# Graph layer: 30 tiles of source rows by single DMAs from two queues, bulk loads on ScalarE's queue, 391 picks instead of 400

## Chip, cores and metric

One core of a Trainium2 chip. The metric is the device time of the kernel in microseconds, as the median of several executions; a profiled execution of the kernel before, with its own time, is read besides.

## What is computed

One message-passing layer of a graph network with 6250 nodes, 200,000 edges (sorted by target node), and 64 features:

```python
w = silu(edge_attr @ W1 + b1) @ W2 + b2              # 200000 x 9
h_src = x[src]                                       # 200000 x 64, a gather
msg = einsum('ef,em,fmg->eg', h_src, edge_sh * w, W_tp)
agg = segment_sum(msg, dst, N) / sqrt(E / N)
emb = silu(c_noise[:, None] @ Wn1 + bn1) @ Wn2 + bn2
gamma, beta = split(emb, 2)
out = layernorm(x + agg * (1 + gamma) + beta)
```

## The kernel before

The edges are cut into 1563 tiles of 128, and 16 tiles make a block (98 blocks, the last one of 11 tiles). For a tile, a window matmul (line 728, in `windows`) multiplies the 128 source rows, as weights, with the weighted spherical harmonics spread over 7 nodes of a window. So every tile needs its 128 rows of `x`, 256 bytes each, with an edge on each partition. There are three ways to get them:

- *Gather*: GpSimd's indirect DMA (line 126, in `gather`), one instruction for a tile. It fetches 1158 tiles.
- *Pick*: TensorE (line 683, in `pick`). The table `x` lies in SBUF as two f32r halves; a one-hot matrix of the source numbers (`hots`, line 668 on VectorE, from keys `kr` that are loaded with a bulk DMA) multiplies it in 14 matmuls of 448 columns, and VectorE masks and reduces the result (lines 693, 696). 400 tiles: five in every ninth block, four in the others (`picked`).
- *Rows one by one*: ScalarE's queue issues a DMA for each row (line 154, in `load_rows`), with the address from a register. One tile in every 16th block, five tiles in all (`APG`), eight rows in a block.

The loop over `i` is written out by hand, and each engine runs its instructions in that order. In iteration `i` TensorE picks for block `i + 1` and, in `middle(i)`, runs the first layer of block `i + 2` (`hidden`, line 609), the second layer of block `i + 1` (`second`, line 633) and the windows of block `i`. GpSimd gathers for block `i + 2` behind marks ("beats") in TensorE's matmuls. Every fourth block is a finishing block (23 of them): two output blocks are normalized, with a square root on ScalarE (line 1039, with its table load) behind that block's rows; the next iteration begins with the placing of sums (line 813), the copy of the carry on ScalarE (line 819), `yt` on VectorE (line 822), and then the first layer.

SyncE's queue carries the bulk loads: at the top of odd iterations the edge attributes `ea` (512 KB for two blocks), harmonics `sh` (144 KB) and keys `kr` (320 KB), every fourth iteration also the node scalars `cb` and the store of two finished blocks:

```python
if i % LB == 1 and i + 1 + LB < NBLK:
    load(i + 1 + LB)
    load_keys(i + 1 + LB)
if i % 4 == 3 and i + 1 < NJ:
    gate_load(i + 1)
```

Each DMA counts on a semaphore from one pool for SyncE and ScalarE, and a new DMA on a semaphore first waits for the one before it there.

## Time and profile before

| what | value |
|---|---|
| three runs | 1475.52, 1476.37, 1476.50 us; median 1476.37 |
| profiled execution | 1476.88 us, its span 1474.5 us |
| TensorE (PE) busy | 1458.9 us, 99% of the span |
| VectorE (DVE) busy | 1257.2 us, 85% |
| GpSimd (POOL) busy | 1097.9 us, 74% |
| ScalarE (ACT) busy | 504.9 us, 34% |
| DMA | 98.27 MB, 67 GB/s mean |

The span runs from the first to the last instruction; the 2.4 us between it and the execution's time lie outside of it. A row of the timeline has start, duration, engine, line, operation and operands, then the idle time in front of it and what ended it. PE is the matmul pipe, PEld the weight loads beside it; ACTq and SPq are DMA issues of ScalarE's and SyncE's queues, which are not counted as busy. Matmuls overlap, so the chain (each piece up to where the next one takes over) tells what a stretch of them costs, not their durations.

### The profile page before, as it was taken

The numbers are of one execution on the slowest core, as the hardware profiler recorded it, in microseconds if no ns is written. First come the engines' busy times: TensorE is split into PE (matmuls) and PEld (weight loads), VectorE is DVE, ScalarE is ACT, GpSimd is POOL, SyncE is SP. The second block draws the span as 40 slices with busy tenths as digits, with TensorE's granted clock in tenths as the row PEclk, the third lists the DMA queues.
The fourth block names the chain that finished last, engine by engine and source line by source line (L and its number), as shares of the span: only waits on it lengthen the run. The fifth ranks groups of instructions, "written<-read, shape, count | busy, mean of one in ns | idle before, by whom it ended". The sixth has DMA issues, their size and how long they took to land.

```text
span 1474.5 us, 32845 instructions
## 1 busy us (share of the span) xinstructions
PE 1458.9 (99%) x12002; PEld 1266.0 (86%) x12002; DVE 1257.2 (85%) x2222; ACT 504.9 (34%) x1413; POOL 1097.9 (74%) x1167
## 2 busy tenths in 40 slices
PE   7999999999999999999999999999999999999998
PEld 6888888888888888888888888888888888888886
DVE  8988898798888888979879898888798888987886
ACT  5332333242333333333424233333242333333333
POOL 7777777777777777777777777777777777777773
PEclk9999999999999999999999999999999999999999
DMA  7413222221222212312222122122221222222211
GB/s 214 105 55 87 59 75 60 68 75 41 75 68 60 75 42 74 83 45 74 58 64 72 39 76 71 50 74 57 62 73 40 74 65 56 75 56 64 57 28 23
DMA packets 85439, 98.27 MB, mean 67 GB/s; under 512 B 32100, under 2 KB 46646, under 8 KB 85270
## 3 DMA queue, kind: packets, MB, share of 16 engines
q1 hardware_dynamic: 46358, 56.29, 12.9%
q0 software_dynamic: 37056, 38.02, 11.5%
q8 instruction: 98, 1.61, 0.4%
q10 hardware_dynamic: 1856, 1.77, 0.4%
q14 instruction: 71, 0.58, 0.1%
HBM read 94.24 MB, written 1.75 MB: 65 GB/s over the span
## 4 chain that ended last, share of the span: by engine, by line
PE 95%; DVE 3%; DMA 1%; SPq 1%; issue 0%; POOL 0%; ACT 0%; POOLq 0%; DVEq 0%
PE pxw L683 75%; PE pzw L728 7%; PE p L609 4%; PE p L633 4%; PE p L797 3%; DVE hot_k L668 1%; PE p L860 1%; PE p L813 1%; PE p L828 1%; SPq L435 1%; DVE xm L693 0%; DVE hs L696 0%; PE pzw L609 0%; PE p L803 0%; DMA out_dram<-o 0%
## 5 line engine op out<-in xcount | busy, mean ns | idle before, releaser
L126 POOL DMA_INDIRECT hs<-in_x_dram,src_i x1158 | 1096.6, 947 | 355.9 <-issue 158.2
L683 PE MATMUL pxw<-xs_w,hot_k 128*128 128x448 f32 x5600 | 1165.1, 365 | 1.5 <-DVE hot_k L668 1.5
L683 PEld LDWEIGHTS pxw<-xs_w,hot_k 128*128 128x128 f32 x5600 | 1036.2, 188 | 78.3 <-ACT xs_w L351 2.3
L693 DVE SCALAR_TENSOR_TENSOR xm<-li,jl,pxw 128x448 f32<-128x448 f32 x400 | 271.0, 678 | 175.2 <-PE pxw L683 174.2
L668 DVE TENSOR_TENSOR hot_k<-kr,pxw 128x896 fp32r<-128x896 f16 x393 | 416.0, 1079 | 0.0
L696 DVE TENSOR_REDUCE hs<-xm 128x64 f32<-128x448 f32 x400 | 248.2, 620 | 13.8
L637 ACT ACTIVATE p2s<-p,b2c 128x256 f32<-128x256 f32 x98 | 46.5, 474 | 599.4 <-PE p L633 577.8
L744 ACT COPY ztw<-pzw 64x140 f32<-64x140 f32 (+1 forms) x778 | 208.8, 268 | 8.5 <-PE pxw L728 0.5
L728 PEld LDWEIGHTS pzw<-a,hs 128*64 128x64 f32 x3106 | 101.1, 138 | 29.5 <-issue 23.8
L653 DVE TENSOR_TENSOR a<-oh,p 128x1008 f32<-128x1008 f32 x98 | 118.0, 1204 | 3.3
L728 PE MATMUL pzw<-a,hs 128*64 128x63 f32 x3106 | 111.2, 224 | 0.1
L624 ACT ACTIVATE st<-pzw,b1c 128x256 f32<-128x256 f32 x196 | 82.3, 471 | 1.2
L620 ACT ACTIVATE st<-p,b1c 128x512 f32<-128x512 f32 x98 | 67.1, 685 | 38.1 <-PE p L797 33.4
L819 ACT COPY carry<-p 128x128 f32<-128x128 f32 x46 | 12.3, 266 | 167.2 <-PE p L813 165.6
L609 PE MATMUL p<-ea,w1bd 32*64 32x256 f32 x784 | 66.5, 402 | 0.9 <-DVE yt L822 0.9
L609 PE MATMUL pzw<-ea,w1bd 32*64 32x256 f32 x784 | 66.5, 402 | 0.0
L633 PE MATMUL p<-st,w2p 128*32 128x256 f32 x784 | 62.6, 391 | 0.6 <-DVE a L653 0.6
L648 DVE TENSOR_TENSOR p<-p,sh 128x72 f32<-128x72 f32 x196 | 47.3, 241 | 6.7
L633 PEld LDWEIGHTS p<-st,w2p 128*32 128x32 f32 x784 | 15.5, 107 | 37.9 <-issue 37.2
L797 PE MATMUL p<-ztw,wtc 128*64 128x224 f32 x440 | 46.5, 357 | 0.0
L644 DVE STREAM_TRANSPOSE p<-p2s 128x256 f32<-128x256 f32 x98 | 44.3, 452 | 0.0
L797 PEld LDWEIGHTS p<-ztw,wtc 128*64 128x64 f32 x440 | 29.6, 136 | 17.1 <-issue 9.1
(187 smaller groups left out, 499.1 us busy)
## 6 DMA issues: line engine op xcount, KB each, us to landing
ea<-in_ea_dram SPq DMA_DIRECT2D x48, 512.0 KB
hs<-in_x_dram,src_i POOLq DMA_INDIRECT x1158
kr<-kd SPq DMA_DIRECT2D x48, 320.0 KB
apart<-in_x_dram ACTq DMA_DIRECT2D x640, 0.2 KB
sh<-in_sh_dram SPq DMA_DIRECT2D x49, 144.0 KB
cb<-cn_d SPq DMA_DIRECT2D x12, 128.0 KB
out_dram<-o SPq DMA_DIRECT2D x23, 64.0 KB
dst_i<-in_dst_dram SPq DMA_DIRECT2D x1, 768.0 KB
```

The lines of the kernel that those rows point to most:

```text
L126: d = nc.gpsimd.indirect_dma_start(out=hs[g][:, t - g * KB, :], out_offset=None, in_=x, in_offset=bass.IndirectOffsetOnAxis(ap=src_i[:, t: ...
L609: mm = nc.tensor.matmul(half[q][s * H:(s + 1) * H].rearrange("p (c t e) -> p c t e", c=4, t=2), w1bd[q * D:(q + 1) * D, (q % 2) * H:(q % 2 ...
L624: nc.scalar.activation(st[g][:, 2 + q], pzw[q][:, 2 * P:], AF.Silu, bias=b1c)
L633: mm = nc.tensor.matmul(p2[g][c * D:(c + 1) * D, 0, :].rearrange("p (q e) -> p q e", q=4), w2p, s[:, :, c * 2 * D:(c + 1) * 2 * D], start= ...
L653: nc.vector.tensor_mul(a[g], oh_t.pop(g)[:, :, None, :].to_broadcast([P, KB, M, W]), sw.unsqueeze(3).to_broadcast([P, KB, M, W]))
L668: nc.vector.tensor_tensor(hot_k[g, t], keys[:, t, None, :].to_broadcast([P, J, P]), n_p.unsqueeze(2).to_broadcast([P, J, P]), op=ALU.is_equal)
L683: mm = nc.tensor.matmul(px.rearrange("p f l -> p (f l)"), hot_k[g, t][:, h, :], xs[i][:, h].rearrange("p f l -> p (f l)"), start=(h == 0 a ...
L693: nc.vector.scalar_tensor_tensor(xm, li[:, None, :].to_broadcast([P, F, J]), jl[:, c:c + 1], px, op0=ALU.is_equal, op1=ALU.mult)
L696: read_by[g, t] = nc.vector.tensor_reduce(hs[g][:, tiles(g) - q + t, :], xm, AX.X, ALU.add)
L728: mm = nc.tensor.matmul(pz[v][v * F:(v + 1) * F, k // 2].rearrange("p m w -> p (m w)"), apart.pop(g) if g in APG and k0 + k == 0 else hsg[ ...
L744: copy(z[h * F:(h + 1) * F, 0:5 - h, k0 + k:k0 + n:2, :].rearrange("p m k w -> p k m w"), pz[v][v * F:(v + 1) * F, k // 2:(n + 1 - v) // 2 ...
L797: mm = nc.tensor.matmul(pt[h * F:(h + 1) * F].rearrange("p (s k w) -> p s k w", s=2, k=KB), wtc2[:, c, :], z[h][:, :, c], start=(c == 0), ...
```

## The change

Ten tiles instead of five come by ScalarE's rows (every eighth block, 16 rows in a block), 20 tiles by rows that SyncE issues (tile 1 of every fourth block from 16 to 92, 32 rows in a block, begun ten blocks ahead and with three buffers). Rows of each queue count on semaphores of their own, and TensorE waits for the whole tile in front of its window matmul. The bulk loads and stores of the loop move from the top of SyncE's iteration to ScalarE's queue, behind the reads and in front of that iteration's rows. Only two blocks (5 and 53) keep a fifth pick: 391 picks, 1142 gathers.

```diff
-APS = 16
+APS = 8
+SPS, SPA = 4, 10
+SPG = range(16, NBLK - 2, SPS)
+SPR = P // SPS
...
-    return Q - 2 if g == 0 else 2 if g == NBLK - 1 else Q - (g % 9 != 5)
+    return Q - 2 if g == 0 else 2 if g == NBLK - 1 else Q - (g % 48 != 5)
...
-            due[g] = list(range(g * KB + (g in APG), g * KB + tiles(g) - picked(g)))
+            due[g] = [g * KB + k for k in range(tiles(g) - picked(g)) if not (k == 0 and g in APG or k == 1 and g in SPG)]
...
-        row_a = keep.tile([len(APG), P], I32)
+        row_a = keep.tile([len(APG) + len(SPG), P], I32)
+        fetched = [tc.alloc_semaphore(f"fetched{k}") for k in range(2)]
...
-                nc.scalar.dma_start(apart[g][e0 + k:e0 + k + 1].bitcast(U8), x8[bass.ds(vs[k], 4 * F)].unsqueeze(0))
+                d = nc.scalar.dma_start(apart[g][e0 + k:e0 + k + 1].bitcast(U8), x8[bass.ds(vs[k], 4 * F)].unsqueeze(0))
+                tc.no_tile_sem_insts.add(d.ins.name)
+                tc.add_to_no_dep_group(f"apart{g}", d.ins)
+                d.then_inc(fetched[APG.index(g) % 2], 16)
+        landed = [tc.alloc_semaphore(f"landed{k}") for k in range(3)]
+        def load_lone(i):
+            g = (i + SPA - SPG[0]) // SPS * SPS + SPG[0]
+            if g not in SPG:
+                return
+            e0 = (i + SPA - SPG[0]) % SPS * SPR
+            if e0 == 0:
+                lone[g] = gath.tile([P, F], F32, tag="lone", name=f"lone{g}", bufs=3)
...
+            for k in range(SPR):
+                d = nc.sync.dma_start(lone[g][e0 + k:e0 + k + 1].bitcast(U8), x8[bass.ds(vs[k], 4 * F)].unsqueeze(0))
...
+                d.then_inc(landed[SPG.index(g) % 3], 16)
...
-            cn_j = temp.tile([NJ, P], F32)
+            cn_j = xb.rearrange("p j f -> p (j f)")[0:NJ, NJ * F - P:]
...
+                    if g in APG and k0 + k == 0:
+                        m = APG.index(g)
+                        w = nc.tensor.wait_ge(fetched[m % 2], (m // 2 + 1) * P * 16)
+                        tc.declare_fence(w.ins, group=f"apart{g}")
+                    if g in SPG and k0 + k == 1:
+                        m = SPG.index(g)
+                        w = nc.tensor.wait_ge(landed[m % 3], (m // 3 + 1) * P * 16)
+                        tc.declare_fence(w.ins, group=f"lone{g}")
...
-                if i % LB == 1 and i + 1 + LB < NBLK:
-                    load(i + 1 + LB)
-                    load_keys(i + 1 + LB)
-                if i % 4 == 3 and i + 1 < NJ:
-                    gate_load(i + 1)
                 while tables:
                     tables.pop()()
-                while stores:
-                    stores.pop(0)()
+                load_lone(i)
...
                 for f in reads:
                     f()
+                if i % LB == 1 and i + 1 + LB < NBLK:
+                    load(i + 1 + LB, nc.scalar)
+                    load_keys(i + 1 + LB, nc.scalar)
+                if i % 4 == 3 and i + 1 < NJ:
+                    gate_load(i + 1, nc.scalar)
+                while stores:
+                    stores.pop(0)(nc.scalar)
                 load_rows(i)
```

TensorE between the windows of block 22 and the next first layer, where block 23 is picked (`hot_k_1` to `hot_k_4` are its tiles 1 to 4, `hot_k_0` is tile 0 of block 24). Before:

```order
L728 MATMUL pzw_90<-a_4373,hs_3533 64x63 x8
L683 MATMUL pxw_93<-xs_w,hot_k_1_4294 128x448 x14
L683 MATMUL pxw_91<-xs_w,hot_k_2_4308 128x448 x14
L683 MATMUL pxw_92<-xs_w,hot_k_3_4418 128x448 x14
L683 MATMUL pxw_93<-xs_w,hot_k_4_4439 128x448 x14
L683 MATMUL pxw_91<-xs_w,hot_k_0_4466 128x448 x2
```

The same place in the change:

```order
L768 MATMUL pzw_90<-a_5995,hs_4577 64x63 x8
L715 MATMUL pxw_92<-xs_w,hot_k_1_5915 128x448 x14
L715 MATMUL pxw_93<-xs_w,hot_k_2_5929 128x448 x14
L715 MATMUL pxw_91<-xs_w,hot_k_3_6070 128x448 x14
L715 MATMUL pxw_92<-xs_w,hot_k_0_6214 128x448 x2
```

One stretch of 14 matmuls is gone; this happens in ten blocks, and in block 53 one is added.

ScalarE from the last first-layer activations of block 39 on (`apart` is the tile that gets single rows). Before:

```order
L624 ACTIVATE st_7688<-pzw_89,b1c 128x256
L624 ACTIVATE st_7688<-pzw_90,b1c 128x256
L149 TENSOR_LOAD row_a
L154 DMA apart_6640<-in_x_dram 1x256 x8
```

The same place in the change:

```order
L656 ACTIVATE st_11454<-pzw_89,b1c 128x256
L656 ACTIVATE st_11454<-pzw_90,b1c 128x256
L597 DMA ea_11515<-in_ea_dram 128x2x512
L600 DMA sh_11516<-in_sh_dram 128x2x144
L621 DMA kr_11519<-kd 128x1280
L532 DMA cb_11521<-cn_d 64x512
L556 DMA out_dram<-o_11313 128x2x64
L153 TENSOR_LOAD row_a
L158 DMA apart_9687<-in_x_dram 1x256 x16
```

Five bulk DMAs now stand in front of the rows, and there are 16 rows instead of eight. On SyncE, in turn, the loop holds nothing but register loads (line 175) and 32 row DMAs (line 180) in a block, and two early stores of keys:

```order
L272 DMA kd<-kt 120x128 x2
L175 TENSOR_LOAD row_a
L180 DMA lone_1367<-in_x_dram 1x256 x32
L175 TENSOR_LOAD row_a
L180 DMA lone_1367<-in_x_dram 1x256 x32
```

The bulk loads that stood there before are gone from this engine.

## Rows read from the trace of the kernel before

**Rows 1.** The page, part 1 (busy us, share, instructions) and part 4 (chain).

```profile
PE 1458.9 (99%) x12002; PEld 1266.0 (86%) x12002; DVE 1257.2 (85%) x2222; ACT 504.9 (34%) x1413; POOL 1097.9 (74%) x1167
...
PE 95%; DVE 3%; DMA 1%; SPq 1%; issue 0%; POOL 0%; ACT 0%; POOLq 0%; DVEq 0%
```

**Rows 2.** Groups: shapes, count, busy us, mean ns, idle before and its releasers.

```profile
L683 PE MATMUL pxw<-xs_w,hot_k 128*128 128x448 f32 x5600 | 1165.1, 365 | 1.5 <-DVE hot_k L668 1.5
L126 POOL DMA_INDIRECT hs<-in_x_dram,src_i x1158 | 1096.6, 947 | 355.9 <-issue 158.2 <-PE pxw L683 92.1 <-DMA hs<-in_x_dram,src_i 58.5
L728 PEld LDWEIGHTS pzw<-a,hs 128*64 128x64 f32 x3106 | 101.1, 138 | 29.5 <-issue 23.8 <-DMA hs<-in_x_dram,src_i 3.7
```

**Rows 3.** Waits: waiter <- releaser, us in total, times, longest us.

```profile
POOL hs L126 <- issue: 158.2, 519, 0.3
ACT var L1039 <- DVE var L1038: 70.9, 23, 4.9
```

**Rows 4.** Timeline at block 4: its last gather, its first window matmuls (start, us).

```profile
80.36 0.94 POOL L126 DMA_INDIRECT hs<-in_x_dram,src_i  x1 [0.30 <-DMA hs<-in_x_dram,src_i]
...
86.77 1.15 PE L728 MATMUL pzw<-a,hs 128*64 128x63 f32 x32
```

**Rows 5.** Timeline at the end: the last gather, first window matmul of block 97.

```profile
1453.42 0.94 POOL L126 DMA_INDIRECT hs<-in_x_dram,src_i  x1 [0.30 <-issue]
...
1464.44 0.24 PE L728 MATMUL pzw<-a,hs 128*64 128x63 f32 x1
```

**Rows 6.** The chain by time, 1020 to 1100 us: runs of pick matmuls.

```profile
1028.61 14.21 PE pxw L683 x70
...
1061.03 11.41 PE pxw L683 x56
```

**Rows 7.** Timeline of ScalarE and its queue, block 38 (finishing), from the last rows.

```profile
601.88 2.18 ACTq L154 DMA_DIRECT2D apart<-in_x_dram  x7
604.09 1.28 ACT L1039 ACT_TABLE_LOAD   x1 [2.08 <-DMA apart<-in_x_dram]
608.07 0.30 ACT L1039 ACTIVATE var<-var,eps 128x2 f32<-128x2 f32 x1 [2.69 <-DVE var L1038]
608.47 0.27 ACT L819 COPY carry<-p 128x128 f32<-128x128 f32 x1
```

**Rows 8.** Timeline of SyncE's queue: two bulk loads in a row.

```profile
610.18 0.42 SPq L565 DMA_DIRECT2D ea<-in_ea_dram  x1
610.65 0.47 SPq L568 DMA_DIRECT2D sh<-in_sh_dram  x1
```

**Rows 9.** Timeline behind them: `yt` on VectorE, first-layer matmul on TensorE.

```profile
609.59 0.28 DVE L822 TENSOR_TENSOR yt<-p,carry 128x128 f32<-128x128 f32 x1
...
610.39 0.43 PE L609 MATMUL p<-ea,w1bd 32*64 32x256 f32 x2
```

**Rows 10.** ScalarE: copy in block 37; block 39's rows; next instruction.

```profile
587.53 0.33 ACT L806 COPY rt<-p 128x224 f32<-128x224 f32 x1
...
616.41 0.46 ACTq L154 DMA_DIRECT2D apart<-in_x_dram  x1
...
626.00 0.47 ACT L637 ACTIVATE p2s<-p,b2c 128x256 f32<-128x256 f32 x1 [8.78 <-DMA ea<-in_ea_dram]
```

**Rows 11.** Windows of 4 us: sum, busy by engine, TensorE clock, DMA share, GB/s.

```profile
610.00:614.00 4.00, 4.00 (x66) 2.75 (x65) 3.97 (x5) 2.20 (x3) 2.94 (x4) 1.00 0.73 208
...
618.00:622.00 4.00, 4.00 (x22) 3.75 (x21) 3.44 (x5) 0.00 (x0) 3.09 (x4) 1.00 0.19 35
622.00:626.00 4.00, 4.00 (x46) 2.90 (x46) 3.93 (x7) 0.00 (x0) 3.09 (x4) 1.00 0.80 238
```

**Rows 12.** VectorE at the start of block 38: first one-hots of new keys.

```profile
594.35 2.08 DVE L668 TENSOR_TENSOR hot_k<-kr,pxw 128x896 fp32r<-128x896 f16 x2
```

**Rows 13.** Timeline at 680 us: a row from ScalarE, a bulk load from SyncE.

```profile
680.04 0.24 ACTq L154 DMA_DIRECT2D apart<-in_x_dram  x1
680.10 0.34 SPq L589 DMA_DIRECT2D kr<-kd  x1
```

More of the change, by code (lines that the diff above doesn't have):

```diff
@@ L153, in load_rows @@
             for k in range(n):
-                nc.scalar.dma_start(apart[g][e0 + k:e0 + k + 1].bitcast(U8), x8[bass.ds(vs[k], 4 * F)].unsqueeze(0))
+                d = nc.scalar.dma_start(apart[g][e0 + k:e0 + k + 1].bitcast(U8), x8[bass.ds(vs[k], 4 * F)].unsqueeze(0))
+                tc.no_tile_sem_insts.add(d.ins.name)
+                tc.add_to_no_dep_group(f"apart{g}", d.ins)
+                d.then_inc(fetched[APG.index(g) % 2], 16)
+        lone = {}
+        landed = [tc.alloc_semaphore(f"landed{k}") for k in range(3)]
[6 more added lines that the diff above has]
+                lone[g] = gath.tile([P, F], F32, tag="lone", name=f"lone{g}", bufs=3)
+            r = len(APG) + SPG.index(g)
+            _, vs = nc.values_load_multi_w_load_instructions(
+                row_a[r:r + 1, e0:e0 + SPR], engines=[mybir.EngineType.SP],
+                min_val=0, max_val=4 * F * (NPAD - 1),
+                skip_runtime_bounds_check_because="src is below N, as for the gathers")
+            for k in range(SPR):
+                d = nc.sync.dma_start(lone[g][e0 + k:e0 + k + 1].bitcast(U8), x8[bass.ds(vs[k], 4 * F)].unsqueeze(0))
+                tc.no_tile_sem_insts.add(d.ins.name)
+                tc.add_to_no_dep_group(f"lone{g}", d.ins)
+                d.then_inc(landed[SPG.index(g) % 3], 16)
         pace = {}
@@ L392, in setup @@
             nc.vector.tensor_copy(lo, lo_i)
-            row_f = temp.tile([P, len(APG)], F32)
-            nc.vector.tensor_scalar(row_f, src_i[:, APG[0] * KB:NBLK * KB:APS * KB], 4.0 * F, None, op0=ALU.mult)
+            row_f = temp.tile([P, len(APG) + len(SPG)], F32)
+            nc.vector.tensor_scalar(row_f[:, 0:len(APG)], src_i[:, APG[0] * KB:NBLK * KB:APS * KB], 4.0 * F, None,
+                                    op0=ALU.mult)
+            nc.vector.tensor_scalar(row_f[:, len(APG):], src_i[:, SPG[0] * KB + 1:SPG[-1] * KB + 2:SPS * KB], 4.0 * F,
+                                    None, op0=ALU.mult)
             pick(0, 1)
             gather(1, 2, read_by[0, 1])
-            p_row = pzw[0][0:len(APG), 0:P]
+            p_row = pzw[0][0:len(APG) + len(SPG), 0:P]
             nc.tensor.transpose(p_row, row_f, ident)
@@ L495, in gnn_resnorm_kernel, with gate_load @@
         cb = {}
-        def gate_load(j0):
+        def gate_load(j0, queue=nc.sync):
             nj = min(4, NJ - j0)
             cb[j0] = loads.tile([H, 4, P], F32, tag="cb", name=f"cb{j0}", bufs=2)
-            nc.sync.dma_start(cb[j0][:, :nj].rearrange("h j p -> h (j p)"), rows(cn_v[j0 * P:(j0 + nj) * P], H))
+            queue.dma_start(cb[j0][:, :nj].rearrange("h j p -> h (j p)"), rows(cn_v[j0 * P:(j0 + nj) * P], H))
         def gate_hidden(j0):
@@ L523, in store @@
                 o = end()
-                stores.append(lambda: nc.sync.dma_start(out_v[:, j0:j1, :], o))
+                stores.append(lambda queue=nc.sync: queue.dma_start(out_v[:, j0:j1, :], o))
             ends.extend([middle, store])
@@ L553, in gnn_resnorm_kernel, with load @@
         ea_t, sh_t, oh_t, kr_t, st, a, zs = {}, {}, {}, {}, {}, {}, {}
-        def load(g):
+        def load(g, queue=nc.sync):
             n = min(LB, NBLK - g)
@@ L564, in part @@
             def part(a0, a1):
-                nc.sync.dma_start(e[:, a0:a1, :], ea[g + a0:g + a1].rearrange("g p c -> p g c"))
+                queue.dma_start(e[:, a0:a1, :], ea[g + a0:g + a1].rearrange("g p c -> p g c"))
             def rest():
-                nc.sync.dma_start(s[:, :n].rearrange("p g k m -> p g (k m)"), sh[g:g + n].rearrange("g p c -> p g c"))
+                queue.dma_start(s[:, :n].rearrange("p g k m -> p g (k m)"), sh[g:g + n].rearrange("g p c -> p g c"))
             if g == 0:
@@ L584, in near, with load_keys @@
                 oh_t[g + i] = o[:, i * KB:(i + 1) * KB, :]
-        def load_keys(g):
+        def load_keys(g, queue=nc.sync):
             n = min(LB, NBLK - g)
             kr = loads.tile([P, LB, Q, P], F16, tag="kr", name=f"kr{g}", bufs=2)
-            nc.sync.dma_start(kr[:, 0:n].rearrange("p g t e -> p (g t e)"),
+            queue.dma_start(kr[:, 0:n].rearrange("p g t e -> p (g t e)"),
                               rows(kd[g * Q:(g + n) * Q, :].rearrange("c e -> (c e)"), P))
@@ L727, in windows @@
                     v = k % 2
+                    if g in APG and k0 + k == 0:
[6 more added lines that the diff above has]
+                        tc.declare_fence(w.ins, group=f"lone{g}")
                     mm = nc.tensor.matmul(pz[v][v * F:(v + 1) * F, k // 2].rearrange("p m w -> p (m w)"),
-                                          apart.pop(g) if g in APG and k0 + k == 0 else hsg[:, k0 + k, :], ag[:, k0 + k].rearrange("p m w -> p (m w)"),
+                                          apart.pop(g) if g in APG and k0 + k == 0 else
+                                          lone.pop(g) if g in SPG and k0 + k == 1 else hsg[:, k0 + k, :], ag[:, k0 + k].rearrange("p m w -> p (m w)"),
                                           start=True, stop=True)
```

## The prediction

> **What bounds the kernel now.** I read four views in this order: the page, the groups of instructions, the chain that ended last, and the timeline at places where engines hand over. On the page TensorE is busy 99% of the span, and the chain is 95% TensorE [rows 1]. So the kernel is a queue of matmuls, and the largest part of it is the picks: 5600 matmuls of line 683, 14 for each of 400 picks [rows 2].
>
> A second engine stands almost as high. GpSimd is shown 74% busy, but its gathers are 947 ns long and 355.9 us of idle time lies in front of 1158 of them, 0.307 us each [rows 2]; its largest wait is never longer than 0.3 us [rows 3]. That gap belongs to every gather, so a gather costs 0.947 + 0.307 = 1.254 us and the queue of GpSimd takes 1158 x 1.254 = 1452 us of 1474.5. Both engines are full, and a tile can be moved off TensorE only if GpSimd doesn't get it. That is what bounds the change: nine picks leave, and 25 more tiles come by single rows, so GpSimd loses 16 gathers too.
>
> How near is GpSimd to being late? In block 4 its last gather ended at 80.36 + 0.94 = 81.30 and the window matmuls that need it began at 86.77: a margin of 5.5 us [rows 4], and all waits of those matmuls' weight loads for gathers come to 3.7 us in the whole run [rows 2]. For block 97 the margin was 1464.44 - 1454.36 = 10.1 us [rows 5].
>
> **The change part by part.**
>
> *Nine picks fewer.* In ten blocks (14, 23, 32, 41, 50, 59, 68, 77, 86, 95) the fifth pick goes, in block 53 one is added. In the chain 70 matmuls in a row took 14.21 us and 56 took 11.41 [rows 6]: 2.80 us for the 14 of a pick, 0.200 us each. All of it lies on the chain: 9 x 2.80 = **25.2 us less**. The other price from the same rows, 11.41/56 = 0.204 us, would give 9 x 2.85 = 25.7; I take the difference, since it leaves out what happens once per stretch. VectorE loses one-hot, masking and reduction of nine tiles; it is not the bound there, so I count nothing.
>
> *GpSimd.* 1142 gathers instead of 1158: 16 x 1.254 = 20.1 us less. TensorE gains 25.2, so the margin at block 97 shrinks from 10.1 to about 5.0. That is 0.5 us under the margin that block 4 shows to be enough. Cost: 0 if a gather lands in 5 us, up to 0.5 if it needs all of the 5.5; I take 0. The cover is thin: if it were gone, each further microsecond of GpSimd would be one of the kernel.
>
> *Rows by SyncE.* 20 tiles x 128 = 2560 row DMAs. ScalarE's rows go every (2.18 - 0.23)/6 = 0.326 us [rows 7]; SyncE's bulk DMAs every 0.47 [rows 8]. A tile of 128 rows is due every four blocks, 4 x 1450/98 = 59.2 us. At 0.326 it takes 42 us, at 0.47 it takes 60.2: a loss of 1 us per tile in the worse case, against tiles begun up to 12 blocks ahead. With the bulk loads gone nothing urgent stands behind a waiting row on SyncE. Cost 0 at both ends; a gain is excluded, as SyncE is not on the chain.
>
> *Waits on TensorE.* 30 new semaphore waits in front of window matmuls. The nearest row: in 98 blocks the weight loads of the windows sat idle 23.8 us by issue, each block with some eight waits [rows 2]: 23.8/98/8 = 0.03 us a wait, 0.9 us for 30. Below, 0: the weight loads run beside matmuls. Above, if each of the 30 cost as much as a block's eight: 30 x 0.24 = 7.3. I take **0.9**, by the row of the same place.
>
> *Sixteen rows instead of eight on ScalarE.* 8 x 0.326 = 2.61 us more per block, from block 9 to 88. The tight place is a block in which two output blocks are finished (23 of them [rows 3]): behind the rows stand the table load for the square root, the root, and the copy of the carry. In block 38 the table load began at 604.09 and the root then waited 2.69 us for VectorE [rows 7]. The rows eat 2.61 of it, 0.08 is left; the carry copy, done at 608.74, was needed at 609.59, so 0.85 more is left, and from `yt` (609.87) to the first-layer matmul that waits for it (610.39) another 0.52 [rows 9]. Sum 1.45 us of cover for a cost of about nothing; I take 0, with the register load of 16 values (in no row) inside the cover.
>
> *Bulk loads on ScalarE.* They leave SyncE, where they ran early, and now go out in odd blocks behind the reads. In block 39 that is five DMAs at 0.47 and 16 rows: from 616.41, 2.4 + 5.5 us gives 624.3, and the next ScalarE instruction started at 626.00 [rows 10]: hidden. The bytes are tighter. Keys, `ea` and `sh` are 976 KB and may start at 587.6, right behind the `rt` copy [rows 10]. `ea` and `sh`, issued at 610.18 and 610.65 [rows 8], moved within a stretch of 4 us at 208 GB/s, and keys with another `ea` at 238, of which 35 is what gathers alone move [rows 11]. So 976 KB (999,424 bytes) take 4.9 us (203 GB/s) to 5.8 us (173; that stretch holds the time from issue to first byte too), and the keys land by 593.4. VectorE first needs them at 594.35 [rows 12]: 0.95 us early. Cost 0 now; what is late next is VectorE, and through `yt` TensorE.
>
> *Setup* gets a 20-column operation and one shared buffer: below 0.3 us, nothing.
>
> **The sum.** -25.2 + 0.9 = -24.3. The profiled execution took 1476.88 us (span 1474.5), so 1452.6 by its own time. Its time is 0.5 above the median of the three runs, 1476.37; against that, **1452.1 us**.
>
> **What could hold the rows up.** When SyncE issued keys at 680.10 while ScalarE issued a row at 680.04, the row took 0.24 us instead of 0.23 [rows 13]: two queues issue side by side at the price of one. [...]
>
> **The rivals.**
>
> 1. *GpSimd sets the pace.* If the gathers must end as far ahead of the last windows as they do now (10.1 us), only the 16 gathers count: 1476.4 - 20.1 = **1456.3 us**. For it: the constant gaps, the full queue. Against: block 4's 5.5 us were enough.
> 2. *Late keys.* The keys stand behind 656 KB on ScalarE's queue. If they land L later than I think, VectorE stands still at the one-hots, in order, and in the 23 finishing blocks `yt` comes late: TensorE loses L less the cover of 0.95 + 0.52 = 1.5 us. It decides at L = 1.5 + 24.3/23 = 2.6; at 4 it costs 23 x 2.5 = 57 us and gives **1509 us**, slower than before. Against: 976 KB at a measured rate.
> 3. *Rows of two queues hold each other up.* Each ScalarE row 0.23 longer, 16 of them 3.7 us, less the cover of 1.45: 2.2 us in the 20 finishing blocks with rows: 44 us, **1496 us**. It decides at 1.45 + 24.3/20 = 2.7 us of delay per block, 0.17 per row. For it: two streams of rows have not run beside each other so far. Against it: the row at 680.04.
>
> **How the numbers follow.** Forecast 0.80, GpSimd 0.09, late keys 0.05, rows in each other's way 0.05, gain lost in some other way 0.01. Small forms of the second and third (under a microsecond in each finishing block) still leave it faster; I put 0.02 of their 0.10 there, and 0.02 to no change. About 0.2% (3 us) is what a measurement of this kernel can tell from no change. Faster 0.91, same 0.03, slower 0.06. The range: at the low end picks at 2.85, waits free and a microsecond of scatter as the three runs have: 1476.4 - 25.7 - 1.0 = 1449.7; at the high end rival 1 with the same scatter, 1457.3. The full price of the waits (7.3) would lie one microsecond above it and is left out, with rivals 2 and 3.
>
> **What would show it.** Line of the picks: 5474 matmuls, still 99% TensorE, and a span near 1450. Weight loads of the windows waiting for gathers: a few microseconds; if tens, rival 1. One-hots on VectorE waiting for a DMA, and first-layer matmuls waiting for `yt`: rival 2. Row DMAs of 0.4 us and more on ScalarE, and table loads that start beyond the readiness of the root's input: rival 3. Windows waiting for the tiles of SyncE would mean that its rows cost over 0.5 us. The prediction is wrong if the picks fall by 25 us and the span doesn't.

## The result and the profile after

The changed kernel takes **1449.76 us** (median of four runs, 1449.34 to 1450.10) where the kernel before takes 1476.43 (four runs, 1475.52 to 1478.41). The ratio is 0.9817, interval 0.9800 to 0.9834. Applied to the 1476.37 us of the forecast that is 1449.4: 2.7 us under the forecast and 0.3 under the low end of its range. The direction and the main mechanism were right; the size was short, by a term that was put at nothing and by one that was put at 0.9 us and measured 0.

The profiled execution took 1450.1 us, its span is 1448.3. The page of the changed kernel, its head, the chain by engine, and three of its costliest groups (busy time and mean ns of one, then idle time and what ended most of it):

```profile
PE 1433.0 (99%) x11876; PEld 1242.1 (86%) x11876; DVE 1235.9 (85%) x2196; ACT 502.0 (35%) x1413; POOL 1082.8 (75%) x1151
...
PE 97%; DVE 1%; DMA 1%; SPq 1%; ACTq 0%; issue 0%; ACT 0%; DVEq 0%
...
L129 POOL DMA_INDIRECT hs<-in_x_dram,src_i x1142 | 1081.5, 947 | 350.3 <-issue 143.4
L715 PE MATMUL pxw<-xs_w,hot_k 128*128 128x448 f32 x5474 | 1139.6, 365 | 1.5 <-DVE hot_k L700 1.5
...
L768 PEld LDWEIGHTS pzw<-a,hs 128*64 128x64 f32 x3056 | 101.1, 138 | 27.5 <-issue 23.7
```

They answer to [rows 1, 2]. TensorE is still the bound at 99%. Picks are now 5474 matmuls, 126 fewer, and GpSimd's gathers are 1142 with the same 947 ns and the same gap (350.3/1142 = 0.307 us): GpSimd still gathers without a pause. The weight loads of the windows sat idle 23.7 us by issue where it was 23.8 before, with 30 more waits in front of them.

Where the 26.2 us of the two spans (1474.5 and 1448.3) went can be read block by block: an interval into a block runs from the first window matmul of the block before it to its own first one. TensorE's timeline from block 22 to block 23, in the kernel before:

```profile
356.96 1.15 PE L728 MATMUL pzw<-a,hs 128*64 128x63 f32 x32
358.04 11.88 PE L683 MATMUL pxw<-xs_w,hot_k 128*128 128x448 f32 x58
...
373.71 1.15 PE L728 MATMUL pzw<-a,hs 128*64 128x63 f32 x32
```

and in the changed kernel:

```profile
354.24 1.15 PE L768 MATMUL pzw<-a,hs 128*64 128x63 f32 x32
355.32 9.08 PE L715 MATMUL pxw<-xs_w,hot_k 128*128 128x448 f32 x44
...
368.18 1.15 PE L768 MATMUL pzw<-a,hs 128*64 128x63 f32 x32
```

Fourteen matmuls fewer in a row are 11.88 - 9.08 = 2.80 us. The last gather of GpSimd and the first window matmul of block 97 in the changed kernel:

```profile
1432.83 0.94 POOL L129 DMA_INDIRECT hs<-in_x_dram,src_i  x1 [0.30 <-issue]
...
1438.50 0.24 PE L768 MATMUL pzw<-a,hs 128*64 128x63 f32 x1
```

The windows of block 97 began at 1464.44 before [rows 5] and begin at 1438.50 now, 25.94 earlier:

| where | before, us | now, us | difference |
|---|---|---|---|
| into ten blocks without their fifth pick, as block 23 | 16.75 | 13.94 | ten times -2.79 to -2.81: -28.0 |
| into block 53, one pick more | 15.89 | 18.68 | +2.8 |
| into blocks 31 and 67, where no pick has changed | 14.48, 14.47 | 13.94, 13.94 | -1.07 |
| into block 61, no finishing block | 15.89 | 16.19 | +0.3 |
| from the first window of block 97 to the end | 10.07 | 9.81 | -0.26 |

Every other interval up to block 96 is the same within 0.005 us.

The third line was in no term of the forecast. In the waits of TensorE's matmuls, in the kernel before, the first layer (line 609) waited twice for `yt` of VectorE (columns: waited for, us in total, times, longest):

```profile
PE p L609 <- DVE yt L822: 0.9, 2, 0.5
```

The same view of the changed kernel:

```profile
PE p L641 <- DVE yt L863: 0.2, 1, 0.2
```

Of the ten blocks that lose their fifth pick, 32 and 68 are those whose fifth one-hot VectorE makes in a finishing iteration, in which it also normalizes two output blocks. There it was late with `yt`, in front of the windows of blocks 31 and 67. The one wait for `yt` that the change has is in front of block 61. In iteration 60, and in no other, VectorE counts values out of range (`n_bad`), and a cast on ScalarE waits 1.40 us for that, before the change as well. So the sixteen rows behind the cast began late, the copy of the carry came right behind them at 923.14, VectorE waited 1.58 us for it, and TensorE 0.22 us for `yt`.

The rows came as forecast. The timeline of ScalarE in a finishing block of the change:

```profile
592.93 5.37 ACTq L158 DMA_DIRECT2D apart<-in_x_dram  x16
598.34 1.28 ACT L1081 ACT_TABLE_LOAD   x1 [5.18 <-issue]
599.63 0.29 ACT L1081 ACTIVATE var<-var,eps 128x2 f32<-128x2 f32 x1
599.83 0.25 ACT L860 COPY carry<-p 128x128 f32<-128x128 f32 x1
```

and SyncE's rows in the same microseconds:

```profile
592.81 1.83 SPq L180 DMA_DIRECT2D lone<-in_x_dram  x6
```

Sixteen rows take 5.37 us on ScalarE; its other work starts right behind them, and the root starts without the 2.69 us wait that it had in [rows 7]. SyncE's six rows beside them take 1.83 us, (1.83 - 0.23)/5 = 0.32 us apart. The last row of each of SyncE's tiles was issued 97 to 128 us ahead of the tile's window.

### The profile page after: what moved, and what is told of

The parts are those of the page before. It is cut to its first block, busy times and chain, and to the rows that moved or that the text cites. A ratio compares the mean times of both kernels' runs of the same rounds, so it can differ in the third digit from the quotient of the medians.

```text
span 1448.3 us, 38930 instructions
## 1 busy us (share of the span) xinstructions
PE 1433.0 (99%) x11876; PEld 1242.1 (86%) x11876; DVE 1235.9 (85%) x2196; ACT 502.0 (35%) x1413; POOL 1082.8 (75%) x1151
## 4 chain that ended last, share of the span: by engine, by line
PE 97%; DVE 1%; DMA 1%; SPq 1%; ACTq 0%; issue 0%; ACT 0%; DVEq 0%
PE pxw L715 75%; PE pzw L768 7%; PE p L665 4%; PE p L641 4%; PE p L838 3%; PE p L901 1%; PE p L854 1%; PE p L869 1%; SPq L467 1%; DVE hot_k L700 0%; PE pzw L641 0%; PE p L844 0%; ACTq L158 0%; DMA out_dram<-o 0%; PE p L821 0%
## 5 line engine op out<-in xcount | busy, mean ns | idle before, releaser
L129 POOL DMA_INDIRECT hs<-in_x_dram,src_i x1142 | 1081.5, 947 | 350.3 <-issue 143.4
L715 PE MATMUL pxw<-xs_w,hot_k 128*128 128x448 f32 x5474 | 1139.6, 365 | 1.5 <-DVE hot_k L700 1.5
L715 PEld LDWEIGHTS pxw<-xs_w,hot_k 128*128 128x128 f32 x5474 | 1012.3, 188 | 76.5 <-ACT xs_w L380 1.9
L725 DVE SCALAR_TENSOR_TENSOR xm<-li,jl,pxw 128x448 f32<-128x448 f32 x391 | 265.0, 678 | 168.2 <-PE pxw L715 167.2
L700 DVE TENSOR_TENSOR hot_k<-kr,pxw 128x896 fp32r<-128x896 f16 x384 | 406.3, 1079 | 0.0
L728 DVE TENSOR_REDUCE hs<-xm 128x64 f32<-128x448 f32 x391 | 242.6, 620 | 13.5
L768 PEld LDWEIGHTS pzw<-a,hs 128*64 128x64 f32 x3056 | 101.1, 138 | 27.5 <-issue 23.7
L860 ACT COPY carry<-p 128x128 f32<-128x128 f32 x46 | 11.8, 257 | 155.7 <-PE p L854 149.2
```

Source lines behind the costliest of these rows:

```text
L129: d = nc.gpsimd.indirect_dma_start(out=hs[g][:, t - g * KB, :], out_offset=None, in_=x, in_offset=bass.IndirectOffsetOnAxis(ap=src_i[:, t: ...
L700: nc.vector.tensor_tensor(hot_k[g, t], keys[:, t, None, :].to_broadcast([P, J, P]), n_p.unsqueeze(2).to_broadcast([P, J, P]), op=ALU.is_equal)
L715: mm = nc.tensor.matmul(px.rearrange("p f l -> p (f l)"), hot_k[g, t][:, h, :], xs[i][:, h].rearrange("p f l -> p (f l)"), start=(h == 0 a ...
L725: nc.vector.scalar_tensor_tensor(xm, li[:, None, :].to_broadcast([P, F, J]), jl[:, c:c + 1], px, op0=ALU.is_equal, op1=ALU.mult)
L728: read_by[g, t] = nc.vector.tensor_reduce(hs[g][:, tiles(g) - q + t, :], xm, AX.X, ALU.add)
L768: mm = nc.tensor.matmul(pz[v][v * F:(v + 1) * F, k // 2].rearrange("p m w -> p (m w)"), apart.pop(g) if g in APG and k0 + k == 0 else lone ...
```

## The experiments

Eight variants ran beside the kernel before, several of them on more than one chip, and the changed kernel twice more. In the first result and in two further series the kernel before took 1476.4 to 1476.8 us; on three other chips 1786, 1788 and 1808. Unless the text says otherwise, kernels are compared on the same chip. The sections on parts use the first kind of chip; the other kind has a section of its own at the end.

### The change again

> The changed kernel itself, beside the kernel before on the same chip. On a chip where the kernel before takes about 1476 us, every theory expects 1449 to 1451 us, 26 to 27 us less. On a chip where the kernel before takes about 1786 us: if the nine picks are worth their 2.80 us on TensorE there too, 25 us less (1761); if the number of rows that the DMA queues fetch sets the pace there, the change fetches 1172 tiles of rows where the kernel before fetches 1163, so 9/1163 of the time more, 14 us (1800); if the moved bulk loads and the separate semaphores are worth nothing, the same as the run with the bulk loads on SyncE, a ratio of 1.012.

Measured: 1449.46 us against 1476.54, ratio 0.9817 (0.9802 to 0.9832).

### 400 picks: all of the change but the picks

```diff
-    return Q - 2 if g == 0 else 2 if g == NBLK - 1 else Q - (g % 48 != 5)
+    return Q - 2 if g == 0 else 2 if g == NBLK - 1 else Q - (g % 9 != 5)
```

> The change with the 400 picks of the kernel before; rows by SyncE and ScalarE, the moved bulk loads and the separate semaphores stay. Where the kernel before takes about 1476 us: theory (the picks alone are the gain, the thirty waits on TensorE and everything else cost nothing): the kernel before's time within 0.5 us, its two waits for yt before blocks 31 and 67 there as well. The prediction's own sum (each new wait 0.03 us): 0.9 us above the kernel before. Where the kernel before takes about 1787 us: 0.4 to 0.6% above it, as twice before.

Measured: 1476.46 us (11 runs) against 1476.76, ratio 1.0000 (0.9991 to 1.0009). The windows of block 97 begin at 1464.5, where the kernel before has 1464.44. So rows from two queues, the moved bulk loads and 30 waits together cost nothing that can be measured (into blocks 61 and 67 they add 0.3 and 0.1 us in the trace), and bring nothing either: what they buy is room on GpSimd. The forecast's 0.9 us for the waits is below what this ratio can tell (0.09% is 1.3 us), but the trace tells it. The timeline of TensorE in the change, the second layer and the windows behind it, in a block without row tiles and in one with a tile of SyncE:

```profile
602.14 0.64 PE L665 MATMUL p<-st,w2p 128*32 128x256 f32 x8
602.71 1.15 PE L768 MATMUL pzw<-a,hs 128*64 128x63 f32 x32
...
616.38 0.64 PE L665 MATMUL p<-st,w2p 128*32 128x256 f32 x8
616.94 0.27 PE L768 MATMUL pzw<-a,hs 128*64 128x63 f32 x1
616.95 0.27 PE L768 MATMUL pzw<-a,lone 128*64 128x63 f32 x1
```

From the one to the other it is 0.57 us without a wait and 0.56 with one. The windows of blocks 1 to 96 take 1.15 us each, in the 30 blocks with a row tile as in the other 66.

### The picks alone

```diff
 (in the kernel before)
-    return Q - 2 if g == 0 else 2 if g == NBLK - 1 else Q - (g % 9 != 5)
+    return Q - 2 if g == 0 else 2 if g == NBLK - 1 else Q - (g % 48 != 5)
```

> The kernel before with 391 picks and nothing else, so that GpSimd makes 1167 gathers. Where the kernel before takes about 1476 us: theory (GpSimd gathers without a pause in the change and ends 4.67 us ahead of block 97's windows, of which 2.8 us are the landing): 25 more gathers of 1.25 us end 31.2 us later, so the windows of block 97 come 29.3 us later than the change's, and the run takes 1479 to 1481 us; nothing of the 25 us is left. Rival (TensorE is the only bound): the change's 1449.5 us. Where the kernel before takes about 1787 us: 0.5% above it, as twice before.

Measured: 1479.74 us against 1476.76, ratio 1.0020 (1.0010 to 1.0030). Nothing of 25 us is left, and 3 us are lost. The waits of TensorE's matmuls in this variant:

```profile
PE pzw L728 <- issue: 11.8, 9, 3.1
PE pzw L728 <- DMA hs<-in_x_dram,src_i: 10.7, 8, 4.7
```

Windows wait 22.5 us in 17 places: 10.7 us for gathers, and 11.8 that the profile puts down to issue, where the kernel before has neither row. Both engines were full, as the forecast said; only the two parts together make a gain.

### The fifth picks of two finishing blocks moved

```diff
 (in the kernel before)
-    return Q - 2 if g == 0 else 2 if g == NBLK - 1 else Q - (g % 9 != 5)
+    return Q - 2 if g == 0 else 2 if g == NBLK - 1 else Q - ((g - (g in (33, 69))) % 9 != 5 or g in (32, 68))
```

> The kernel before with its fifth picks of blocks 32 and 68 made in blocks 33 and 69 instead; the work is the same to the instruction. Theory (VectorE with a fifth one-hot in a finishing block is late with yt, which costs TensorE 0.54 us before block 31's and 67's windows): 1.1 us less than the kernel before where that takes 1476 us, the wait of the first feature matmul for yt falling from 2 times to none. Rival (those 0.54 us are the fifth pick's own, in whatever block): no difference, within 0.2 us. On a chip where the kernel before takes about 1786 us both expect no difference that can be measured.

Measured: 1475.20 us (11 runs) against 1476.54, ratio 0.9992 (0.9983 to 1.0001): 1.3 us less, by an interval that just reaches no change. The trace decides it: the row of TensorE waiting for `yt` is gone,

```profile
PE pxw L683 <- DVE hot_k L668: 1.5, 2, 1.3
PE p L633 <- DVE a L653: 0.7, 1, 0.7
```

the intervals into blocks 31 and 67 are 13.94 each, as in the change, and the windows of block 97 begin at 1463.27, 1.18 us earlier (1.07 of it in those two intervals). The same picks in another block cost less: the 0.54 us each were VectorE's lateness, not the picks' own.

### The bulk loads back on SyncE

```diff
+                if i % LB == 1 and i + 1 + LB < NBLK:
+                    load(i + 1 + LB)
+                    load_keys(i + 1 + LB)
+                if i % 4 == 3 and i + 1 < NJ:
+                    gate_load(i + 1)
                 while tables:
                     tables.pop()()
...
                 load_lone(i)
...
-                if i % LB == 1 and i + 1 + LB < NBLK:
-                    load(i + 1 + LB, nc.scalar)
-                    load_keys(i + 1 + LB, nc.scalar)
...
                 load_rows(i)
```

(Gate loads and stores are moved back with them.)

> The change with the bulk loads issued by SyncE as before, ahead of its 32 rows of the block. Where the kernel before takes about 1476 us: theory (32 rows take SyncE 12.8 us of a block of 14.8, so a load waits for at most what is left of the rows of the block before): keys come on SyncE less than 3 us late, within the slack, and the time is the change's within 1 us. Rival (the loads queue behind rows as in the run with the loads behind ScalarE's rows, which cost 2.5 us for each of the 47 loads): up to 117 us more than the change. Where the kernel before takes about 1787 us: 0.9 to 1.2% above it, as twice before.

Measured: 1449.88 us, two runs, ratio to the kernel before 0.9819: the change's time. The bulk loads needn't have moved. Its SyncE timeline shows how they fit between the rows of two blocks:

```profile
589.83 5.37 SPq L180 DMA_DIRECT2D lone<-in_x_dram  x17
595.26 0.41 SPq L597 DMA_DIRECT2D ea<-in_ea_dram  x1
595.76 0.45 SPq L600 DMA_DIRECT2D sh<-in_sh_dram  x1
596.30 0.41 SPq L621 DMA_DIRECT2D kr<-kd  x1
```

### The bulk loads behind ScalarE's rows

```diff
+                load_rows(i)
                 if i % LB == 1 and i + 1 + LB < NBLK:
                     load(i + 1 + LB, nc.scalar)
...
-                load_rows(i)
```

> The change with the block's bulk loads issued behind the sixteen rows on ScalarE's queue instead of ahead of them, about 6.2 us later (sixteen rows and a register load). Theory (the bulk loads have more slack than that, so their move was free): the change's time within 1 us. Rival (late keys, priced in the prediction: above 2.6 us late, the one-hots wait): blocks that load keys, 47 of them, lose up to 3.6 us each, up to 170 us more.

Measured: 1566.15 us against 1476.54, ratio 1.0607 (1.0587 to 1.0626): 116.7 us slower than the changed kernel's 1449.46 on the same chip, 116.7/47 = 2.5 us a load. My theory (slack of more than 6 us) fell. The waits in this variant:

```profile
DVE hot_k L700 <- DMA kr<-kd: 172.9, 40, 5.7
...
PE p L641 <- DMA ea<-in_ea_dram: 39.8, 29, 2.3
PE p L641 <- DVE yt L863: 30.4, 21, 1.7
PE pxw L715 <- DVE hot_k L700: 21.2, 29, 1.7
```

This is the second rival of the prediction made real: keys late, one-hots late on VectorE, and TensorE behind them. TensorE's largest wait, though, is for the edge attributes themselves (39.8 us), which that rival did not name. By its price, L less 1.5 us in 23 finishing blocks, 6.2 us late would cost 23 x 4.7 = 108 us; that the size is near is luck, since three of four intervals between blocks grew (by 2.5, 1.9 and 1.3 us from block 10 to 13), not one. In the change the loads stand in front of the rows on the same queue, and no one-hot waits for keys in its trace. The order of those two calls is worth 117 us.

### 389 picks

```diff
-SPG = range(16, NBLK - 2, SPS)
+SPG = range(12, NBLK, SPS)
...
-    return Q - 2 if g == 0 else 2 if g == NBLK - 1 else Q - (g % 48 != 5)
+    return Q - 2 if g == 0 else 2 if g == NBLK - 1 else Q - 1
```

> The change with four picks in every block (389 picks) and 22 lone tiles by SyncE, so that GpSimd still makes 1142 gathers. Theory (TensorE is the bound, a pick is worth 2.80 us, rows cost nothing): 2 x 2.80 = 5.6 us less than the change, 1444 us where the kernel before takes 1476 us. Rival (GpSimd's margin at block 97, 4.74 us in the change, is used up): the last windows wait for gathers, 5.6 less 4.74 is 0.9 us lost, 1445 us. On a chip where the kernel before takes about 1786 us: 2 more tiles of rows, so if rows set the pace there, some 3 us more than the change.

Measured: 1450.62 us against the change's 1449.46 on that chip. Two more picks are gone and the time is 1.2 us longer (five runs, 1449.95 to 1451.01, against 1449.06 to 1450.25). GpSimd's last gather and TensorE's windows of block 97, in the timelines of this variant:

```profile
1433.86 0.94 POOL L129 DMA_INDIRECT hs<-in_x_dram,src_i  x1 [0.30 <-PE pt L821]
```

```profile
1433.88 0.32 PE L826 MATMUL pt<-ident,rt 128*112 128x128 f32 x1 [0.35 <-ACT rt L829]
1436.67 0.34 PE L768 MATMUL pzw<-a,hs 128*64 128x63 f32 x1 [2.47 <-DMA hs<-in_x_dram,src_i]
...
1442.42 0.69 PE L1054 MATMUL py<-last,c 112*128 112x64 f32 x2 [0.34 <-DVE last L1053]
```

TensorE stands still for 2.47 us, the windows begin 1436.67 - 1434.80 = 1.87 us behind the last gather's end, and from there to the last matmul it is 5.75 us. In the changed kernel on that chip the same stretch takes 3.46 us:

```profile
1438.02 0.24 PE L768 MATMUL pzw<-a,hs 128*64 128x63 f32 x1
...
1441.48 0.43 PE L1054 MATMUL py<-last,c 112*128 112x64 f32 x2 [0.33 <-DVE last L1053]
```

The table of stretches shows the granted clock beside it, this variant first and then the change (length, busy us and count of PE, PEld, DVE, ACT, POOL, granted clock of TensorE, DMA share, GB/s):

```profile
1434.00:1440.00 6.00, 3.53 (x31) 3.07 (x31) 1.78 (x8) 1.47 (x6) 0.80 (x1) 0.70 0.06 11
1440.00:1449.00 9.00, 2.77 (x26) 2.33 (x26) 2.65 (x13) 0.82 (x4) 0.00 (x0) 0.50 0.08 18
```

```profile
1434.00:1440.00 6.00, 5.54 (x62) 4.59 (x60) 4.75 (x16) 2.67 (x11) 0.00 (x0) 1.00 0.03 5
1440.00:1448.00 8.00, 1.58 (x26) 1.27 (x25) 3.10 (x15) 0.85 (x4) 0.00 (x0) 0.68 0.10 23
```

The granted clock is 0.70 in the stretch with the stall and 0.50 of full speed behind it, and the first window matmul takes 0.34 us instead of 0.24; in the change TensorE is busy for 5.54 of the 6 us and has 1.00 there, then 0.68. So 5.6 us of picks were paid for with 2.4 of waiting, 2.3 of a slower end, and 1.4 that was lost in the intervals into blocks 12 and 16 (14.74 for 14.23, 14.86 for 14.23) and 13 and 17 (0.12 to 0.13 each); the cause of these last wasn't found.

This also corrects the forecast: from the end of a gather to its landing it is 1.6 to 1.9 us (1.87 here, 1.60 in the variant with the picks alone), so of the margin of 4.67 us that the change has at block 97 on that chip (from the end of the last gather to the first window), 2.8 us are to spare.

### 390 picks and one more tile by SyncE

```diff
-SPG = range(16, NBLK - 2, SPS)
+SPG = range(16, NBLK, SPS)
...
-    return Q - 2 if g == 0 else 2 if g == NBLK - 1 else Q - (g % 48 != 5)
+    return Q - 2 if g == 0 else 2 if g == NBLK - 1 else Q - (g != 5)
```

> The change with a fifth pick in block 5 alone (390 picks) and one more lone tile by SyncE, in block 96, so that GpSimd still makes 1142 gathers. Where the kernel before takes about 1476 us: theory (a pick is 2.80 us of TensorE; GpSimd's spare at block 97 is 4.67 - 2.8 = 1.9 us): windows of block 97 would come 2.80 us earlier, of which 0.9 us waits for the last gather; 1447.6 us, 1.9 less than the change. Rival (as with 389 picks, the wait at the end lets TensorE's clock fall and costs more than it saves): 1449 to 1450 us, no gain. Where the kernel before takes about 1787 us: 1.1% above it, as once before.

Measured: **1447.41 us** (five runs, 1446.48 to 1447.61) against 1476.76, ratio 0.9800 (0.9787 to 0.9814). It is below every run of the changed kernel on chips of this kind (1449.06 to 1450.25), by some 2 us, though never timed beside it on one such chip. The last gather and the first window matmul of block 97:

```profile
1432.45 0.94 POOL L129 DMA_INDIRECT hs<-in_x_dram,src_i  x1 [0.30 <-issue]
...
1436.19 0.24 PE L768 MATMUL pzw<-a,hs 128*64 128x63 f32 x1
```

The margin is 2.80 us and nothing waits: the landing takes less than the 2.8 us I had counted (I had counted from the gather's start). So the expected 1447.6 us met the time, but not its working: no 0.9 us was waited. The whole pick is gained in the interval into block 53, which is 15.89 us where the change has 18.68. In the two profiled executions 0.9 us of it is hidden by the start: the first window comes at 31.77 here, and at 30.88 in the changed kernel that ran beside 389 picks.

### Chips on which the kernel before takes 1786 to 1808 us

The first four variants ran on such a chip (before: 1786.49 us):

> All moves of the change (30 tiles by rows, bulk loads on ScalarE's queue, own semaphores), but the picks as before, 400; 1133 gathers. If TensorE's queue sets the time and rows, waits and moved loads are free, the nine picks bring their time back: 1449.8 + 25.2, and the stops of TensorE for late sums in blocks 31 and 67 (1.1 us by the windows' starts) come back too: 1475 to 1476.5, no change against before. If the moves themselves bring the 2 us that the sum missed: 1473 to 1474.5. If GpSimd set the pace in the change, 9 gathers less than there would give 1438.

> The kernel before with 391 picks and nothing else; 1167 gathers. If GpSimd's queue is as full as its gaps of 0.307 us say, its last gather ends at 1454.4 + 9 x 1.254 = 1465.6 and the last windows follow 2 to 5 us later: 1480 to 1484 in all, slower than before by some 5 us. If only TensorE's queue counts: 1450.

> The change with the loop's bulk loads and stores back on SyncE's queue, in front of its rows. SyncE's rows take 12.8 us of a block of 14.8, the loads some 1.2 more, so if nothing else is in the way it is the same time as the change, 1449 to 1451. If the waits of the loads for free buffers (up to 19 us each on that queue before) hold up the rows behind them, the tiles by rows come late and the time rises: 1455 to 1500, with windows waiting for tiles from SyncE.

> The change with its rows on the common pool of semaphores, as before, and no waits of their own on TensorE. Each DMA waits for the one eight places before it in the pool. If a row lands in about 2 us, 8 rows in 2 us for both queues together is 0.25 us per row, SyncE's 32 rows then take over 15 us with the register load and fall behind a block of 14.8, and ScalarE's 16 rows take longer than the cover of 1.45 us in finishing blocks: slower than the change by 20 us or more, 1470 to 1600. If the own semaphores are of no account: 1449 to 1451.

The fourth has this edit, for both queues. Its bulk loads stay on ScalarE's queue, as in the change (the kernel that ran has no other edit, though the last expectation of it says that they are back on SyncE):

```diff
-                d = nc.sync.dma_start(lone[g][e0 + k:e0 + k + 1].bitcast(U8), x8[bass.ds(vs[k], 4 * F)].unsqueeze(0))
-                tc.no_tile_sem_insts.add(d.ins.name)
-                tc.add_to_no_dep_group(f"lone{g}", d.ins)
-                d.then_inc(landed[SPG.index(g) % 3], 16)
+                nc.sync.dma_start(lone[g][e0 + k:e0 + k + 1].bitcast(U8), x8[bass.ds(vs[k], 4 * F)].unsqueeze(0))
...
-                        w = nc.tensor.wait_ge(landed[m % 3], (m // 3 + 1) * P * 16)
```

A second chip (before: 1788.17 us) took three of them again, and the variant with 390 picks:

> The change with the 400 picks of the kernel before; rows by SyncE and ScalarE, the moved bulk loads and the separate semaphores stay. Where the kernel before takes about 1476 us: theory (the picks alone are the gain, the thirty waits on TensorE and everything else cost nothing): the kernel before's time within 0.5 us, its two waits for yt before blocks 31 and 67 there as well. The prediction's own sum (each new wait 0.03 us): 0.9 us above the kernel before.

> The kernel before with 391 picks and nothing else, so that GpSimd makes 1167 gathers. Theory (GpSimd gathers without a pause in the change and ends 4.67 us ahead of block 97's windows, of which 2.8 us are the landing): 25 more gathers of 1.25 us end 31.2 us later, so the windows of block 97 come 31.2 - (4.67 - 2.8) = 29.3 us later than the change's, and the run takes about 1479 us, up to 1481 with a slower end; nothing of the 25 us is left. Rival (TensorE is the only bound): the change's 1449.5 us.

> The change with the bulk loads issued by SyncE as before, ahead of its 32 rows of the block. Theory (32 rows take SyncE 12.8 us of a block of 14.8, so a load waits for at most what is left of the rows of the block before): keys come on SyncE less than 3 us late, within the slack, and the time is the change's within 1 us. Rival (the loads queue behind rows as in the run with the loads behind ScalarE's rows, which cost 2.5 us for each of the 47 loads): up to 117 us more than the change.

> The change with a fifth pick in block 5 alone (390 picks) and one more lone tile by SyncE, in block 96, so that GpSimd still makes 1142 gathers. Theory (a pick is 2.80 us of TensorE; GpSimd's spare at block 97 is 4.67 - 2.8 = 1.9 us, and one gather fewer is not had, since the pick left out is one more): windows of block 97 2.80 us earlier, the last gather as late as before, so 2.8 - 1.9 = 0.9 us of it waits for the last gather; 1447.6 us, 1.9 less than the change. If the landing takes less than 2.8 us: 1446.7. Rival (as with 389 picks, the wait at the end lets TensorE's clock fall and costs more than it saves): 1449 to 1450 us, no gain.

and a third one (before: 1808.49 us) the changed kernel and the fourth variant:

> The changed kernel itself. Where the kernel before takes about 1476 us: 1449 to 1450 us again. Where it takes about 1787 us: as the change with the bulk loads on SyncE, which was 0.9 and 1.2% slower there, so 1803 to 1809 us.

> The change with its rows on the semaphores of the common pool and the bulk loads at the top of SyncE's iteration, as the kernel before has both. A row then waits for an earlier DMA on its semaphore, and TensorE for the rows by the pool's counts. Where the kernel before takes about 1787 us this took 6.7% more than it, with TensorE waiting 126 us in 11 windows for lone tiles from block 53 on. Where it takes about 1476 us: theory (the rows' own semaphores are needed: the pool makes windows wait for rows of later tiles): the same 11 waits of 8 to 16 us, about 100 us more than the change, 1550 us. Rival (those waits belong to the other chips' pauses): within 5 us of the change.

| variant | ratio to the kernel before | interval |
|---|---|---|
| 400 picks | 1.0056; 1.0042 | 1.0033 to 1.0080; 1.0025 to 1.0058 |
| the picks alone | 1.0053; 1.0053 | 1.0029 to 1.0076; 1.0034 to 1.0072 |
| bulk loads on SyncE | 1.0121; 1.0093 | 1.0097 to 1.0145; 1.0073 to 1.0113 |
| 390 picks | 1.0110 | 1.0093 to 1.0127 |
| **the changed kernel** | 1.0109 | 1.0090 to 1.0128 |
| shared semaphores | 1.0667; 1.0679 | 1.0637 to 1.0698; 1.0642 to 1.0715 |

The expectations that speak of a kernel bound by TensorE can't be judged here. On the one such chip that ran it the change is **1.1% slower**, as the last expectation of it had it. Its two halves, everything but the picks and the picks alone, lose 0.4 to 0.6% and 0.5% on the other two chips, which add up to about that. The page of the changed kernel there looks different:

```profile
PE 1615.5 (88%) x11876; PEld 1356.0 (74%) x11876; DVE 1247.4 (68%) x2196; ACT 508.2 (28%) x1413; POOL 1082.3 (59%) x1151
...
L129 POOL DMA_INDIRECT hs<-in_x_dram,src_i x1142 | 1081.0, 947 | 722.9 <-PE pxw L715 261.9
```

and its timeline of GpSimd:

```profile
804.44 0.94 POOL L129 DMA_INDIRECT hs<-in_x_dram,src_i  x1 [1.31 <-PE p L665]
806.11 0.94 POOL L129 DMA_INDIRECT hs<-in_x_dram,src_i  x1 [0.72 <-remote]
807.84 0.94 POOL L129 DMA_INDIRECT hs<-in_x_dram,src_i  x1 [0.79 <-PE pzw L768]
```

A gather takes the same 947 ns, but the idle time in front of them is 722.9 us instead of 350.3, here in pauses of 0.7 to 1.3. TensorE is busy 88%, and its windows begin behind short stops of their own (78.2 us in 136 places, put down to issue). SyncE's 32 rows of a block take 15.0 us where they take 10.4 on the first kind of chip, and the mean granted clock of TensorE is 0.94 where it is 1.00 there. The largest part of GpSimd's pauses, 261.9 us, ends with TensorE's picks, whose marks release the gathers; so neither engine is full, and the trace doesn't show which of them holds the other up. Why these chips pause, what a pick less is worth there, and why the rest of the change costs 0.4 to 0.6% isn't settled. The change isn't the cause of the pauses: the kernel before is as slow there, and with 391 picks and no other edit it has 662.8 us of idle time in front of its gathers. Its own trace wasn't taken on such a chip.

One thing is plain on these chips too. With shared semaphores TensorE's waits read

```profile
PE pzw L752 <- DMA lone<-in_x_dram: 124.9, 12, 18.2
```

and the timelines of SyncE and of TensorE at block 56

```profile
1095.86 9.45 SPq L175 DMA_DIRECT2D lone<-in_x_dram  x27
```

```profile
1106.34 0.34 PE L752 MATMUL pzw<-a,lone 128*64 128x63 f32 x1 [11.15 <-DMA lone<-in_x_dram]
```

That is 125 us in 12 windows, where the changed kernel has no such row; the variant is 1930.93 us against the change's 1828.01 on the same chip, 103 us more. The tile's last row was issued at 1105.31 and its window began 1.0 us behind it: TensorE waited for the tile's own rows, which SyncE issued too late, and not for rows of later tiles, as the last expectation has it. SyncE's 32 rows take 17.1 us in this variant instead of 15.0, since they stand behind other DMAs on the semaphores that they share (SyncE waits 36.7 us for earlier rows of its own, 30.4 for ScalarE's rows and 27.1 for edge attributes), and it falls behind, as the first expectation of this variant said. Its last row comes 92 us ahead of the window in block 16, 24 us in block 40, and 1.0 to 1.4 us from block 48 on; in the changed kernel on this chip it stays 118 us ahead or more. So on this chip the rows need semaphores of their own, to keep SyncE ahead. What this costs on the other kind of chip, where 32 rows take 10.4 us, wasn't measured.

## Why the prediction was right and where it was short

- **Nine picks, -25.2.** Right to a tenth: each of eleven intervals moved by 2.79 to 2.81 us. The difference of two stretches of the chain was the right price; 2.85 us a pick would have been 0.4 us too much in all.
- **"VectorE ... is not the bound there, so I count nothing."** This is the step that failed. VectorE is not the bound of the kernel, but in two blocks a fifth one-hot fell together with two output blocks to finish, and TensorE waited for `yt`. That is 1.07 us in the trace of the change, and 1.07 again in that of the run with those two picks moved (1.3 between its medians). The row was in the profile before, the wait of line 609 for `yt`, 0.9 us in 2 places, and blocks 32 and 68 were in my own list of ten. It is the largest of the misses, which add up to 2.5 of the 2.7 us: the waits of the next point come second (0.9), then the time outside of the span and the end (0.6 and 0.26), less 0.3 that block 61 lost.
- **Thirty waits, +0.9.** Measured 0: the run with 400 picks has the kernel before's time, and windows begin 0.56 us behind the second layer with a wait, 0.57 without. The nearest row was an average of idle time over waits that may each have been free; the lower bound of the forecast, 0, was the value.
- **GpSimd, 0.** Right: margin at block 97 forecast 5.0, measured 4.7, no window waits. My bound by block 4 (5.5 us) was too careful: 2.8 us are enough, as the run with 390 picks shows. The first rival is the run with the picks alone and the one with 389 picks; in the change it didn't come.
- **Rows by SyncE and sixteen on ScalarE, 0.** Right, but for the interval into block 61: behind the cast that waits for VectorE the rows began late, and 0.3 us were lost. The forecast took a finishing block to be the tight place, and this one isn't.
- **Rows of two queues side by side, 0.** Right. ScalarE's rows go every 0.325 us (median) beside SyncE's and went every 0.326 alone [rows 7]; SyncE's go every 0.32. The median row DMA is 0.235 us long on ScalarE's queue (0.228 in the kernel before) and 0.228 on SyncE's, over 3840 rows. No run shows the 0.23 us that the third rival adds to a row of ScalarE; the median is 0.007 longer.
- **Bulk loads in time, 0.** Right, and on ScalarE's queue the order in front of the rows is what makes it so: behind them it is 117 us. On SyncE's queue they are in time as well, as the run with them there shows.
- **The end.** 0.26 us of the span behind block 97 and 0.6 of the time outside of the span (1476.88 - 1474.5 = 2.4 before, 1.8 now) were in no term.

Together: -25.2 - 1.07 + 0.3 - 0.26 = -26.2 for the span, and with the 0.6 outside of it -26.8 between the two profiled executions, where -24.3 was forecast.

## What to carry to other kernels

When two engines are full, price a move for both: the picks alone lost 3 us and the rows alone gained nothing, but together they gave 27. When work is taken from an engine that "isn't the bound", look in the waits of the bounding engine for places where it is late all the same, and see whether the removed work stands there. A queue's order can be worth more than its load (117 us for swapping two calls), and a gain of this kind should be timed on more than one chip: here it was -1.8% on one kind and +1.1% on the one chip of the other kind that ran it.

## What was not expected of the hardware

- Three chips ran the same kernel before 21 to 22% slower (1786 to 1808 us against 1476), with a mean granted clock of 0.94 to 0.96 where the others have 1.00. The changed kernel's gathers take the same 947 ns there, with twice the idle time between them (722.9 us against 350.3).
- With a stall of 2.47 us on TensorE close to the end (389 picks) its granted clock fell from 1.00 to 0.50, and the rest of its work took 5.75 instead of 3.46 us; the stall cost almost twice its length. With the picks alone, behind a stall of 4.74 us, the same work took 5.75 us too.
- A gather's data are used 1.6 to 1.9 us behind the end of its instruction where TensorE waits for them (389 picks, picks alone), less than any margin that the kernel before shows; its smallest is the 5.5 us of block 4.
